# Four graph layers on one core: paired norm statistics, score dots from a PSUM copy, and new prices and offsets for the planner

## The chip, the core and the metric

The kernel runs on one core of a Trainium2 chip. The metric is the device time of one execution in microseconds; the time before is the median of three runs, 3304.65 us (3302.43 to 3311.59). A core has five instruction queues, which are named here as in the profile: PE (TensorE, matmuls; PEld are its weight loads), DVE (VectorE), ACT (ScalarE), POOL (GpSimd) and SP (SyncE, which issues the DMAs). SBUF is the working memory; PSUM is the memory that matmuls write, and DVE and ACT can read and write it too. The kernel uses PSUM as eight buffers of 128 x 512 float32.

## The reference, cut to what matters

`x` has the shape (128, 64, 512): 128 graphs of 64 nodes with 512 features. All numbers are float32. Each layer ends in a residual and a layer norm.

```python
def _layernorm(x, axis=-1, eps=1e-5):
    m = jnp.mean(x, axis=axis, keepdims=True)
    v = jnp.var(x, axis=axis, keepdims=True)
    return (x - m) / jnp.sqrt(v + eps)

# layer 0
out = deg[None, :, None] * (mi + b) + jnp.einsum('ij,bjo->bio', a, mj)
# layer 1: four attention heads, then one over the joined heads, then a feed-forward with its own norm
h = jax.nn.elu(_gat_heads(enc_inputs, adj, W_heads, a_heads))
...
out = jax.nn.elu(_gat_heads(h, adj, W_out[None], a_out[None])[:, 0])
ffn = jnp.maximum(out @ w1 + b1, 0.0) @ w2 + b2
y = ffn + out
...
return (y - mu) / jnp.sqrt(var + LN_EPS) * ln_gamma + ln_beta
# layers 2 and 3
Wh = jnp.einsum('bnd,de->bne', x, W)
e_src = jnp.einsum('bnd,d->bn', Wh, a_src)
e_dst = jnp.einsum('bnd,d->bn', Wh, a_dst)
logits = e_src[:, :, None] + e_dst[:, None, :]
logits = jnp.where(logits >= 0, logits, NEG_SLOPE * logits)
...
attn = jax.nn.softmax(logits, axis=-1)
attn = jnp.nan_to_num(attn, nan=0.0)
out = jnp.einsum('bnm,bmd->bnd', attn, Wh)
# the whole
x = _layernorm(x + layer(x, ...), axis=-1)      # for each of the four layers
```

## The kernel before, in words

The 128 graphs are 64 tiles of 128 rows (two graphs a tile). Two tiles make a *pair* (T = 2), so there are 32 pairs, p = 0 to 31, and 30 of them go in groups of two for the heads' matmuls. A pair's `x` stays in SBUF from the first layer to its output. Weights that are used again and again are streamed from DRAM (tiles named `ws_...`).

Matrix products are done by a seven-product scheme, `strassen` and `seven`: products gather in PSUM tiles `stx`, `sty` (and `stz` for the heads) and DVE adds them to the result in SBUF. Its operand sums (`s`, `s_o`, `s_y`, `t`) are POOL's. `seven` calls `whole(t)` when tile t of the result is whole: tile 0 after the fifth product, tile 1 after the seventh. There the norm of that tile begins.

A norm is `moments`, which is `bn_stats` and `bn_aggr` on DVE (tiles `st` and `mv`), then on POOL two operations on one column, the addition of epsilon and the power of -0.5 (tile `rs`). `normalize` adds DVE's shift `sh` = -mean x rs and one ACT instruction that scales and shifts the 128 x 512 tile. `norms` is the norm within layer 1 (its tiles end in `_1i`): moments, two DVE operations over 128 x 512 through a PSUM tile `ng`, then `normalize`.

Attention scores are dot products of a row of `x` with vectors that were multiplied through the weights beforehand, so no product Wh is needed for them. `dots` has DVE do them: for each of two vectors and two tiles one multiply-and-add over 128 x 512 (`tensor_tensor_reduce`, CUSTOM_DVE_ANT_0 in the profile, out to `j`) followed by the read of its accumulator into `f`. The vectors are broadcast to all partitions by DMA (`rows`). `stage_scores` does it for the four heads with four sets of rows, for pairs 2 to 31 (the first two pairs use matmuls); `stage_gat` for layers 2 and 3, for pairs 0 to 30; `stage_project` for `who`, the input of layer 1's second attention. `attention` then makes the softmax; in layers 2 and 3 the reciprocal `r` of the sum is multiplied by `has`, which is 0 for a node without neighbours.

The last pair runs by `stage_last` and `stage_tile`, a tile at a time with plain matmuls. The first six pairs (AHEAD) run layer 0 with plain matmuls too.

What sets the order is a planner. The stages are generators that note instructions (`Plan.note`) without issuing them; `yield 3.0` hands over to other stages for so much planned time. An instruction's rank is its place in the notes plus the offset of its kind from the table `LATER` (a kind is engine and tile, "te:stx"; "/S" is added for the first 11% of the notes, "/E" for the last 7%). `Plan.order` then simulates the five queues with a price for each instruction from `cost`: whenever an engine is free it takes the ready instruction of lowest rank. It also hands out tile buffers, the eight PSUM tiles (tag "b") among them, nearly in the order of the notes (NEAR). What comes out is the fixed order of each queue in the program; on the chip each engine goes through its queue in that order and waits where a result is not there. All instructions are issued by one line of `Plan.play`, L394, so the profile has one line for nearly everything and the tiles' names tell them apart.

Of the kernel before, what the change touches and what calls it, by code (L numbers as in the profile page):

```python
# [12 lines left out]
FP = mybir.dt.float32  # L13
BF = mybir.dt.bfloat16
I32 = mybir.dt.int32
AF = mybir.ActivationFunctionType
# [36 lines left out]
    "gp:aT": -137, "gp:aT/E": 66, "gp:aTg": 160, "gp:aTg/S": 321, "gp:ax": 238, "gp:ax/S": 124,  # L53
    "gp:bones": 54, "gp:bones/S": 51, "gp:fill": -170, "gp:fill/S": 66, "gp:gT": -160,
    "gp:gT/E": -163, "gp:gT/S": 4, "gp:hT": 400, "gp:hT/E": 72, "gp:hT/S": 5, "gp:hid": 64,
    "gp:hid/E": -203, "gp:hid/S": 44, "gp:ident": 138, "gp:ident/S": -93, "gp:mhalf": -400,
    "gp:mhalf/S": 96, "gp:never": 38, "gp:never/S": -5, "gp:o": 22, "gp:o/E": -95, "gp:o/S": 64,
    "gp:raw_W": -282, "gp:raw_W/S": 128, "gp:raw_w": -269, "gp:raw_w/S": -18, "gp:raw_wo": 15,
    "gp:raw_wo/S": 67, "gp:rs": 33, "gp:rs/S": 12, "gp:rs_i": 118, "gp:rs_i/E": -400,
    "gp:rs_i/S": 133, "gp:s": 32, "gp:s/E": -70, "gp:s/S": -46, "gp:s_o/E": -30, "gp:s_y": 75,  # L60
    "gp:s_y/E": -18, "gp:s_y/S": -25, "gp:t": -100, "gp:t/E": 179, "gp:t/S": -36, "gp:wh": -32,
    "gp:wh/S": 103, "gp:x": 43, "gp:x/E": -17, "gp:x/S": 27, "gp:ys": 11, "gp:ys/E": 148,
    "gp:ys/S": -271, "sc:a": -112, "sc:aT": 66, "sc:aT/E": 37, "sc:aT/S": -1, "sc:aT_o": 198,
    "sc:aT_o/E": 54, "sc:aTg": 38, "sc:aTg/E": 89, "sc:aTg/S": 62, "sc:a_h": -85,
    "sc:a_h/S": -114, "sc:ax": 275, "sc:ax/S": -233, "sc:bc": -55, "sc:elu": 278,
    "sc:elu/E": 69, "sc:elu/S": -88, "sc:f": -1, "sc:f/S": 15, "sc:gT": 70, "sc:gT/E": -33,
    "sc:hT": -218, "sc:hT/S": 107, "sc:hid": -42, "sc:hid/E": 137, "sc:o": 37, "sc:o/E": -40,
    "sc:o/S": -12, "sc:oT/E": -89, "sc:sm": -132, "sc:sm/E": -139, "sc:sm_o": -32,
    "sc:sm_o/E": 5, "sc:sm_o/S": 167, "sc:wat/S": 6, "sc:wat_h": 51, "sc:wat_h/S": -87,
    "sc:who": -33, "sc:who/E": 391, "sc:who/S": 29, "sc:x": -84, "sc:x/E": 51, "sc:xT": 14,  # L70
    "sc:xT/S": -265, "sc:ys": 30, "sc:ys/E": -17, "sc:ys/S": -86, "sy:W_last": -77,
    "sy:W_last/E": 157, "sy:adj_i": -224, "sy:adj_i/S": -45, "sy:b_sb": 129, "sy:b_sb/S": -118,
    "sy:beta": 215, "sy:beta/S": 13, "sy:d": 116, "sy:d/S": -6, "sy:d_W": -227, "sy:d_W/S": 130,
    "sy:d_W_T": -156, "sy:d_W_T/S": 60, "sy:d_f": 22, "sy:d_f/S": -11, "sy:d_h": 131,
    "sy:d_w": -353, "sy:d_w/S": -7, "sy:d_w_T": -12, "sy:d_w_T/S": 74, "sy:d_wh_S": -41,
    "sy:d_wh_S/S": 102, "sy:d_wo": -38, "sy:d_wo/S": -274, "sy:d_wo_T": -44, "sy:d_wo_T/S": 30,
    "sy:degb": -15, "sy:degb/S": 34, "sy:dram": -77, "sy:dram/E": -221, "sy:dram/S": -107,
    "sy:over": -119, "sy:over/S": 33, "sy:raw_W": -56, "sy:raw_W/S": 14, "sy:raw_w": -185,
    "sy:raw_w/S": 44, "sy:raw_wo/S": -31, "sy:rows": 93, "sy:rows/E": -108, "sy:rows/S": 25,
    "sy:rows_a": 215, "sy:rows_a/S": -76, "sy:rows_b": 103, "sy:rows_b/E": 40,  # L80
    "sy:rows_b/S": -25, "sy:rows_gamma": -33, "sy:rows_gamma/E": -72, "sy:rows_gamma/S": 16,
    "sy:rows_last": -88, "sy:rows_last/E": -8, "sy:rows_o": 20, "sy:rows_o/E": -138,
    "sy:rows_o/S": 155, "sy:w/S": -7, "sy:w_last": 79, "sy:w_last/E": -36, "sy:wh/S": 172,
    "sy:ws_W": 243, "sy:ws_W/E": -12, "sy:ws_W/S": 36, "sy:ws_W_T": -22, "sy:ws_W_T/E": 221,
    "sy:ws_W_T/S": 60, "sy:ws_w": 10, "sy:ws_w/E": 101, "sy:ws_w/S": 126, "sy:ws_w_T": 216,
    "sy:ws_w_T/E": -21, "sy:ws_w_T/S": -89, "sy:ws_wh/E": -21, "sy:ws_wh/S": -129,
    "sy:ws_wh_S": -11, "sy:ws_wh_S/E": 17, "sy:ws_wh_S/S": 55, "sy:ws_wo": 84, "sy:ws_wo/E": 82,
    "sy:ws_wo/S": 179, "sy:ws_wo_T": -360, "sy:ws_wo_T/E": -40, "sy:ws_wo_T/S": -18, "sy:x": 11,
    "sy:x/S": -43, "te:abd_ps": 3, "te:axp": 53, "te:axp/S": 27, "te:bc": -74, "te:bc/S": 33,
    "te:bc_o": -297, "te:bc_o/E": -9, "te:bc_o/S": -32, "te:fp": 6, "te:gp/E": 2, "te:gp/S": 93,  # L90
    "te:hidp": 76, "te:hidp/E": 16, "te:hidp/S": -39, "te:l": -109, "te:l/S": -1, "te:oTp": 40,
    "te:oTp/E": 137, "te:oTp/S": -205, "te:op": -253, "te:op/E": 178, "te:op/S": -50,
    "te:pt": -15, "te:pt/E": 54, "te:pt/S": -32, "te:pt_o": -73, "te:pt_o/E": -23,
    "te:pt_o/S": -97, "te:stx/E": 6, "te:stx/S": 21, "te:stx_h": -4, "te:stx_h/E": -109,
    "te:stx_o/E": 245, "te:stx_o/S": 10, "te:stx_y": 11, "te:stx_y/S": -26, "te:sty": 2,
    "te:sty/S": -20, "te:sty_h": -47, "te:sty_h/S": -27, "te:sty_o/E": -11, "te:sty_o/S": -29,
    "te:sty_y": -5, "te:sty_y/S": -4, "te:stz_h/E": 21, "te:wap": -29, "te:wap/S": 78,
    "te:wap_h": 279, "te:wap_h/S": -53, "te:xTp": 50, "te:xTp/S": 67, "te:yp/E": 1,
    "te:yp/S": -53, "te:z": -75, "te:z/E": 100, "ve:abd": -232, "ve:abd/S": 135, "ve:adj_f": 28,
    "ve:adj_f/S": 390, "ve:aggr": -6, "ve:aggr/S": 29, "ve:bc": -102, "ve:deg": 119,  # L100
    "ve:deg/S": -123, "ve:degb": 44, "ve:degb/S": 35, "ve:e/E": -129, "ve:e/S": -249,
    "ve:e_o": -169, "ve:e_o/E": 78, "ve:e_o/S": -70, "ve:f/E": 111, "ve:f/S": -25,
    "ve:f_o": -79, "ve:f_o/S": 51, "ve:gT/E": 18, "ve:gT/S": -17, "ve:hT": -8, "ve:hT/S": -210,
    "ve:has": -11, "ve:has/S": -98, "ve:ident": -122, "ve:ident/S": 48, "ve:mask": -266,
    "ve:mask/S": 177, "ve:mv": -35, "ve:mv/E": -83, "ve:mv/S": 86, "ve:mv_i": 209,
    "ve:mv_i/E": 80, "ve:mv_i/S": 142, "ve:mx": -67, "ve:mx/S": 22, "ve:ng": 35,
    "ve:ng/E": -118, "ve:ng/S": 67, "ve:nm/E": -141, "ve:nm/S": 33, "ve:nm_o": 133,
    "ve:nm_o/E": 277, "ve:nm_o/S": -302, "ve:o": 46, "ve:o/E": -35, "ve:o/S": 24,
    "ve:over": -105, "ve:over/S": -138, "ve:r": 91, "ve:r/E": -162, "ve:r/S": 83, "ve:r_o": -29,
    "ve:r_o/E": 45, "ve:r_o/S": 100, "ve:sh/S": 76, "ve:sm": 51, "ve:sm/S": -32, "ve:some": -51,  # L110
    "ve:some/S": -400, "ve:st": 14, "ve:st/E": -400, "ve:st/S": 39, "ve:st_i": -102,
    "ve:st_i/E": -38, "ve:wa": 4, "ve:wa_h": -52, "ve:wa_h/S": -53, "ve:who": 10, "ve:who/E": 4,
    "ve:who/S": -64, "ve:x": -230, "ve:x/E": -11, "ve:x/S": 47,
# [297 lines left out]
def cost(engine, name, args, kw, out):  # L411

    size = size_of(out)
    if engine == "tensor":
        if name == "transpose":
            return size * 0.00085, 0.0

        beside = P * P // math.prod(kw["lhsT"].shape)
        return (
            size * 0.00169 if beside == 1 else 0.208 / beside + 0.0003 * size  # L420
        ), 0.0
    if engine == "sync":
        return 0.06, 0.0015 * size
    if name == "tensor_tensor_reduce":
        return 0.7, 0.0
    if engine == "gpsimd":
        return 0.2 + 0.0021 * size, 0.0
    return 0.17 + (0.0011 if engine == "vector" else 0.00085) * size, 0.0
# [3 lines left out]
def gnn_stack_kernel(  # L432
# [92 lines left out]
    mhalf = cp.tile([P, 1], FP, tag="mhalf", name="mhalf")  # L525
# [268 lines left out]
    def moments(x, name):  # L794

        stats = small.tile([P, 6], FP, tag="stats", name=f"st_{name}")
        mv = small.tile([P, 2], FP, tag="mv", name=f"mv_{name}")
        nc.vector.bn_stats(stats, x)
        nc.vector.bn_aggr(mv, stats)
        rstd = small.tile([P, 1], FP, tag="rstd", name=f"rs_{name}")  # L800
        nc.gpsimd.tensor_scalar(rstd, mv[:, 1:2], EPS, None, ALU.add)
        nc.gpsimd.tensor_tensor(rstd, rstd, mhalf, ALU.pow)
        return mv[:, 0:1], rstd

    def normalize(x, name):

        mean, rstd = moments(x, name)
        shift = small.tile([P, 1], FP, tag="shift", name=f"sh_{name}")
        nc.vector.scalar_tensor_tensor(shift, mean, -1.0, rstd, ALU.mult, ALU.mult)
        nc.scalar.activation(x, x, AF.Identity, bias=shift, scale=rstd)  # L810

    def dots(f, x, rows, name):

        for s in range(2):
            for t in range(T):
                junk = unit.tile([P, D], BF, tag="junk", name=f"j_{name}_{s}_{t}")
                nc.vector.tensor_tensor_reduce(
                    junk, x[:, t, :], rows[:, s, :], 1.0, 0.0, ALU.mult, ALU.add,
                    accum_out=f(s, t),
                )  # L820

# [65 lines left out]
    def attention(f, alpha, mask, fill, has, name, T=T):  # L887
# [27 lines left out]
        if has is not None:  # L915
            nc.vector.tensor_scalar(r, r, has, None, ALU.mult)
# [569 lines left out]
```

## Time and profile before

| what | value |
|---|---|
| median of three runs | 3304.65 us |
| profiled execution, its span | 3308.7 us |
| instructions | 53,418 |
| mean granted clock of TensorE | 0.994 |
| POOL, the two rs operations, 256 each | 353 and 601 ns |
| the same in the inner norm, 64 each | 413 and 639 ns |
| DVE shift sh, 256 | 402 ns |
| ACT normalization of a tile, 256 | 812 ns |
| DVE alpha step of the attention, 128 x 128, layers 2 and 3, and in layer 1's second attention | 489 and 320 ns |
| DVE multiply of e by r, 128 x 128, layers 2 and 3 | 368 ns |
| DMA queue, share of 16 engines' span | 77.5% |

The profiled execution is one run of the program; times of groups are from it alone, and its span is 4 us above the median of the runs. In a line of a group, the two numbers after the bar are the busy time in us and the mean ns of one; then follow the idle time of the engine just before these instructions and what ended most of it. A matmul of float32 shows as two records, so the counts of PE are counts of records. A mean hides a spread: one line can be quick on a quiet stretch and slow on another.

### The profile page before, as it was taken

To read this page: it belongs to the slowest core of one execution; us is meant where nothing else is said; L and a number is where in the kernel's file an instruction comes from. 1 tells how busy PE (TensorE), PEld (TensorE's weight loads), DVE (VectorE), ACT (ScalarE), POOL (GpSimd) and SP (SyncE) were. 2 spreads that over 40 slices of the span, in tenths; PEclk is the share of its full clock that TensorE was granted. 3 is DMA by queue.
4 is the path that set the end of the run, shared out by engine and by line. 5 is a ranking of instruction groups with operands and counts; after the bars stand their busy time and mean duration, and the time that the engine had idled before them with its cause. 6 is when DMAs were issued, how large, how long until landed. Compare 5 with 4: busy or idle time off the path is not lost.

```text
span 3308.7 us, 53418 instructions
## 1 busy us (share of the span) xinstructions
PE 3234.1 (98%) x17860; PEld 2754.2 (83%) x17860; DVE 2313.0 (70%) x5480; ACT 1323.0 (40%) x2986; POOL 1652.5 (50%) x1794
## 2 busy tenths in 40 slices
PE   9999999999999999999999999999999999999997
PEld 5677888888888888888888888888888888878885
DVE  5876767767676776767767677676767767566666
ACT  3434334334433434334344443344344343433343
POOL 6754444455553544644455544555534454545433
PEclk9999999999999999999999999999999999999998
DMA  9896777878778787777878778787787877678772
GB/s 357 299 356 214 241 265 248 287 238 270 246 259 273 242 282 237 256 266 246 281 228 265 260 250 283 235 273 245 263 267 251 281 229 262 197 244 288 259 261 80
DMA packets 380702, 850.47 MB, mean 257 GB/s; under 512 B 42080, under 2 KB 58512, under 8 KB 380432
## 3 DMA queue, kind: packets, MB, share of 16 engines
q1 hardware_dynamic: 380432, 847.07, 77.5%
q8 instruction: 145, 2.38, 0.3%
q14 instruction: 125, 1.02, 0.1%
HBM read 806.13 MB, written 40.78 MB: 256 GB/s over the span
## 4 chain that ended last, share of the span: by engine, by line
PE 89%; DMA 6%; DVE 3%; issue 1%; POOL 1%; ACT 0%; SPq 0%; POOLq 0%; DVEq 0%
PE stx_h L394 13%; PE stx_o L394 12%; PE stx L394 11%; PE sty_o L394 9%; PE sty L394 8%; PE hidp L394 6%; PE stz_h L394 6%; PE sty_h L394 4%; PE yp L394 4%; PE gp L394 3%; DMA ws_wh<-d_wh 3%; PE stx_y L394 3%; PE l L394 3%; PE axp L394 2%; PE sty_y L394 2%; DVE j L394 1%
## 5 line engine op out<-in xcount | busy, mean ns | idle before, releaser
L394 DVE CUSTOM_DVE_ANT_0 j<-x,rows 128x512 bf16<-128x512 f32 x736 | 586.6, 797 | 64.1 <-DMA rows<-d 23.9
L394 POOL TENSOR_SCALAR rs<-mv 128x1 f32<-128x1 f32 x256 | 90.3, 353 | 549.8 <-DVE mv L394 538.0
L394 ACT COPY hT<-stx_h 128x512 f32<-128x512 f32 (+1 forms) x204 | 114.0, 559 | 548.1 <-PE stx_h L394 541.3
L394 ACT ACTIVATE x<-x,sh,rs 128x512 f32<-128x512 f32 x256 | 205.3, 812 | 249.8 <-DVE sh L394 249.3
L394 DVE TENSOR_TENSOR x<-stx,x 128x256 f32<-128x256 f32 x352 | 146.8, 419 | 176.4 <-PE stx L394 175.5
L394 PE MATMUL stx_h<-ys,ws_wh 128*128 128x256 f32 (+1 forms) x1088 | 247.0, 370 | 15.0 <-DMA ws_wh<-d_wh 14.6
L394 PE MATMUL sty_o<-ws_wo,hT 128*128 128x256 f32 x1024 | 246.3, 384 | 2.2 <-DMA ws_wo<-d_wo 2.2
L394 PE MATMUL stx_o<-ws_wo_T,s_o 128*128 128x256 f32 x1024 | 242.7, 380 | 2.3 <-DMA ws_wo_T<-d_wo_T 1.1
L394 PEld LDWEIGHTS stx_h<-ys,ws_wh 128*128 128x128 f32 x1088 | 195.6, 191 | 49.3 <-issue 16.8
L394 PE MATMUL hidp<-oT,w 128*128 128x256 f32 (+1 forms) x1056 | 233.8, 375 | 1.4 <-ACT oT L394 1.4
L394 ACT ACTIVATE elu<-hT 128x512 f32<-128x512 f32 x256 | 154.3, 603 | 187.8 <-DVE hT L394 184.7
L394 PEld LDWEIGHTS sty_o<-ws_wo,hT 128*128 128x128 f32 x1024 | 196.1, 193 | 29.7 <-issue 2.5
L394 PEld LDWEIGHTS hidp<-oT,w 128*128 128x128 f32 x1056 | 196.0, 192 | 28.2 <-ACT oT L394 2.0
L394 PEld LDWEIGHTS stx_o<-ws_wo_T,s_o 128*128 128x128 f32 x1024 | 190.1, 191 | 27.7 <-ACT e L394 1.5
L394 POOL TENSOR_TENSOR hid<-hid 128x256 f32<-128x256 f32 x31 | 22.7, 732 | 362.4 <-ACT hid L394 362.4
L394 DVE SCALAR_TENSOR_TENSOR hT<-elu,hT 128x512 f32<-128x512 f32 x256 | 174.6, 683 | 33.6 <-ACT elu L394 33.1
L394 DVE BATCH_NORM_STATS2 st<-x 128x6 f32<-128x512 f32 x256 | 176.3, 689 | 4.6
L394 POOL TENSOR_TENSOR rs<-rs,mhalf 128x1 f32<-128x1 f32 x256 | 153.9, 601 | 21.3
L394 ACT ACTIVATE elu<-elu 128x512 f32<-128x512 f32 x256 | 149.4, 583 | 6.8
L394 ACT COPY ys<-yp 128x512 f32<-128x512 f32 x256 | 134.3, 602 | 43.6 <-PE yp L394 42.9
L394 DVE SCALAR_TENSOR_TENSOR sh<-mv,rs 128x1 f32<-128x1 f32 x256 | 101.1, 402 | 71.6 <-POOL rs L394 70.8
L394 POOL TENSOR_TENSOR s<-gT 128x256 f32<-128x256 f32 x62 | 49.9, 804 | 200.6 <-DVE gT L394 197.2
(215 smaller groups left out, 7986.4 us busy)
## 6 DMA issues: line engine op xcount, KB each, us to landing
ws_wo_T<-d_wo_T SPq DMA_DIRECT2D x256, 512.0 KB, 4.8
ws_wo<-d_wo SPq DMA_DIRECT2D x192, 512.0 KB, 4.5
ws_wh_S<-d_wh_S SPq DMA_DIRECT2D x272, 256.0 KB, 4.1
ws_W_T<-d_W_T SPq DMA_DIRECT2D x248, 256.0 KB, 3.9
rows<-d_h SPq DMA_DIRECT2D x240, 256.0 KB, 4.2
ws_w_T<-d_w_T SPq DMA_DIRECT2D x104, 512.0 KB, 6.0
ws_wh<-d_wh SPq DMA_DIRECT2D x204, 256.0 KB, 4.8
ws_W<-d_W SPq DMA_DIRECT2D x186, 256.0 KB, 4.3
```

The lines of the kernel that those rows point to most:

```text
L394: getattr(getattr(self.tc.nc, s.engine), name)(*map(real, args), **{k: real(v) for k, v in kw.items()})
```

## The change

Six things are done.

1. `both`, `normalize_both` and `norms_both` are new. A pair's two tiles still get their own `bn_stats` and `bn_aggr` when each is whole, but into one tile `mv`; the epsilon, the power, and the shift are done once, over two columns, when the second tile is there. Then both tiles are normalized, one after the other. Layer 3's two output DMAs are issued after that. `moments` and `normalize` stay for the single tiles, with tiles of the new shape.
2. `seen` is new. It has ACT copy both tiles of `x` to PSUM, and the dots of `stage_scores` (pairs 2 to 31, one copy for all four sets of rows) and of `stage_gat` read `x` from there. `stage_project`'s dots go on reading `who` from SBUF, and `stage_tile`'s reading `x`.
3. `dots` goes over tiles in the outer loop and over the two vectors in the inner one, and its operands change places.
4. In `attention`, the multiplication of `r` by `has` and that of `e` by `r` become one instruction.
5. `cost` has new prices.
6. All of `LATER` is new, with "/M" for the notes between "/S" and "/E"; values lie between -500 and 500 (before: -400 to 400).

```diff
 LATER = {
-    "te:sty/S": -20, "te:sty_h": -47, "te:sty_h/S": -27, "te:sty_o/E": -11, "te:sty_o/S": -29,
...
+    "te:stx": -4, "te:stx/E": -71, "te:stx/M": 3, "te:stx/S": -372, "te:stx_h": -1,
+    "te:stx_h/E": 443, "te:stx_h/M": -18, "te:stx_h/S": -456, "te:stx_o": -34, "te:stx_o/E": -12,
+    "te:stx_o/M": 35, "te:stx_o/S": -25, "te:stx_y": -500, "te:stx_y/E": -367, "te:stx_y/M": 337,
...
 def cost(engine, name, args, kw, out):
 
     size = size_of(out)
+    views = [v for v in kw.values() if isinstance(v, View)]
+    ones = [v for v in [*args, *views] if isinstance(v, View) and math.prod(v.shape[1:]) == 1]
     if engine == "tensor":
...
         beside = P * P // math.prod(kw["lhsT"].shape)
-        return (
-            size * 0.00169 if beside == 1 else 0.208 / beside + 0.0003 * size
-        ), 0.0
+        if beside == 1:
+            return max(0.223, 0.0054 + size * 0.001667), 0.0
+        return (0.125 if beside == 2 else 0.27), 0.0
...
     if name == "tensor_tensor_reduce":
-        return 0.7, 0.0
+        held = any(isinstance(v, View) and v.tile.pool.space is PSUM for v in args)
+        return (0.77 if held else 0.86), 0.0
     if engine == "gpsimd":
-        return 0.2 + 0.0021 * size, 0.0
-    return 0.17 + (0.0011 if engine == "vector" else 0.00085) * size, 0.0
+        return 0.15 + 0.00235 * size + (0.25 if size == 1 else 0.0), 0.0
+    if engine == "scalar":
+        return 0.16 + 0.00085 * size + (0.1 * len(ones) if name == "activation" else 0.0), 0.0
+    return 0.15 + 0.00106 * size + (0.08 if ones else 0.0), 0.0
...
+    def both(x, name, then):
+
+        mv = small.tile([P, T, 2], FP, tag="mv", name=f"mv_{name}")
+
+        def whole(t):
+            stats = small.tile([P, 6], FP, tag="stats", name=f"st_{name}_{t}")
+            nc.vector.bn_stats(stats, x[:, t, :])
+            nc.vector.bn_aggr(mv[:, t, :], stats)
+            if t < T - 1:
+                return
+            rstd = small.tile([P, T], FP, tag="rstd", name=f"rs_{name}")
+            nc.gpsimd.tensor_scalar(rstd, mv[:, :, 1], EPS, None, ALU.add)
+            nc.gpsimd.tensor_tensor(rstd, rstd, mhalf, ALU.pow)
+            then(mv[:, :, 0], rstd)
+        return whole
+
+    def normalize_both(x, name, last=lambda t: None):
+
+        def then(mean, rstd):
+            shift = small.tile([P, T], FP, tag="shift", name=f"sh_{name}")
+            nc.vector.scalar_tensor_tensor(shift, mean, -1.0, rstd, ALU.mult, ALU.mult)
+            for t in range(T):
+                nc.scalar.activation(
+                    x[:, t, :], x[:, t, :], AF.Identity, bias=shift[:, t : t + 1],
+                    scale=rstd[:, t : t + 1],
+                )
+                last(t)
+        return both(x, name, then)
+
     def dots(f, x, rows, name):
 
-        for s in range(2):
-            for t in range(T):
+        for t in range(T):
+            for s in range(2):
                 junk = unit.tile([P, D], BF, tag="junk", name=f"j_{name}_{s}_{t}")
                 nc.vector.tensor_tensor_reduce(
-                    junk, x[:, t, :], rows[:, s, :], 1.0, 0.0, ALU.mult, ALU.add,
+                    junk, rows[:, s, :], x(t), 1.0, 0.0, ALU.mult, ALU.add,
                     accum_out=f(s, t),
                 )
 
+    def seen(x, name):
+
+        got = []
+        for t in range(T):
+            ps = psum.tile([P, D], FP, tag="b", name=f"seen_{name}_{t}")
+            nc.scalar.copy(ps, x[:, t, :])
+            got.append(ps)
+        return lambda t: got[t]
...
+        wide_r = r.unsqueeze(2).to_broadcast(bc3)
         if has is not None:
-            nc.vector.tensor_scalar(r, r, has, None, ALU.mult)
-        nc.vector.tensor_tensor(e, e, r.unsqueeze(2).to_broadcast(bc3), ALU.mult)
+            nc.vector.scalar_tensor_tensor(e, e, has, wide_r, ALU.mult, ALU.mult)
+        else:
+            nc.vector.tensor_tensor(e, e, wide_r, ALU.mult)
...
+    def norms_both(o, x, gamma_sb, name):
+
+        def then(mean, rstd):
+            whole = normalize_both(x, f"1_{name}")
+            for t in range(T):
+                ps = psum.tile([P, D], FP, tag="b", name=f"ng_{name}_{t}")
+                with nc.soon():
+                    nc.vector.scalar_tensor_tensor(
+                        ps, o[:, t, :], mean[:, t : t + 1], gamma_sb, ALU.subtract, ALU.mult
+                    )
+                    nc.vector.scalar_tensor_tensor(
+                        x[:, t, :], ps, rstd[:, t : t + 1], x[:, t, :], ALU.mult, ALU.add
+                    )
+                whole(t)
+        return both(o, f"1i_{name}", then)
...
+        if p >= 2:
+            held = seen(x, f"1_{p}")
...
                 dots(
                     lambda i, t: f[:, s, t * H + 2 * h2 + i : t * H + 2 * h2 + i + 1],
-                    x, r, f"1_{p}_{h2}_{s}",
+                    held, r, f"1_{p}_{h2}_{s}",
                 )
...
-            whole=lambda t: norms(o[:, t, :], x[:, t, :], gamma_sb, f"{p}_{t}"),
+            whole=norms_both(o, x, gamma_sb, f"{p}"),
...
-        dots(lambda s, t: f[:, s, t : t + 1], x, r, f"{name}_{p}")
+        dots(lambda s, t: f[:, s, t : t + 1], seen(x, f"{name}_{p}"), r, f"{name}_{p}")
...
-        def norm(t):
-            normalize(x[:, t, :], f"{name}_{p}_{t}")
+        def last(t):
             if name == "3":
                 nc.sync.dma_start(out=out[ts(p * T + t, P), :], in_=x[:, t, :])
...
-            f"{name}_{p}", 1.8, whole=norm,
+            f"{name}_{p}", 1.8, whole=normalize_both(x, f"{name}_{p}", last),
```

## The prediction

> **What bounds the kernel now.** I read the page's busy times first, then the price of an uninterrupted matmul in the chain of waits, then who TensorE waits for in the middle and at the end, then the groups that the change touches.
>
> ```profile
> span 3308.7 us, 53418 instructions
> PE 3234.1 (98%) x17860; PEld 2754.2 (83%) x17860; DVE 2313.0 (70%) x5480; ACT 1323.0 (40%) x2986; POOL 1652.5 (50%) x1794
> ```
>
> PE is busy for 98% of the span, and the next engine, DVE, for 70%. Busy is not the same as useful, since ends of matmuls are modelled, so I price the work. In the chain of waits these pieces run without a break:
>
> ```profile
> 2692.17 1.73 PE stz_h L394 x8
> 27.77 13.93 PE l L394 x32
> 2723.95 1.78 PE gp L394 x16
> 2677.57 1.99 PE yp L394 x32
> 2697.35 1.02 PE op L394 x8
> ```
>
> One record of 256 columns costs 1.73/8 = 0.216 us, one of 512 columns 13.93/32 = 0.435, a full one of 128 columns 1.78/16 = 0.111, a half-height one (yp, axp) 1.99/32 = 0.062, a quarter one (op) 0.128. The groups by shape count 11,996, 244, 2,223, 3,072 and 256 of them, and 69 small ones at about 0.11: 2594 + 106 + 247 + 191 + 33 + 8 = 3179 us. The span is 3308.7, so 130 us are lost in all. The same count by stage: 0 to 471 us loses 35; 471 to 2670 (eleven double turns of 199.9 us) loses 29; 2670 to 3190 loses 31; the last 119 us lose 34. Waits of TensorE in the middle have one cause, and it is small; the end is a set of short dependences:
>
> ```profile
> PE stx_h L394 <- DMA ws_wh<-d_wh: 11.3, 16, 2.2
> ```
>
> This is all that is listed between 470 and 2670 us (us in total, times, longest). After 3190 us the list is led by
>
> ```profile
> PE bc L394 <- DVE f L394: 4.9, 2, 4.1
> PE pt L394 <- DVE e L394: 1.8, 2, 1.3
> PE gp L394 <- ACT aTg L394: 1.8, 2, 1.1
> ```
>
> So TensorE sets the pace for two thirds of the time with 1.3% to spare (29/2199). Nothing that only relieves DVE, ACT or POOL can win there more than those 29 us. All work of TensorE stays as it is: its matmuls, tiles and weight streams are untouched.
>
> **The change part by part.** First the *score dots*.
>
> ```profile
> L394 DVE CUSTOM_DVE_ANT_0 j<-x,rows 128x512 bf16<-128x512 f32 x736 | 586.6, 797 | 64.1 <-DMA rows<-d 23.9 <-DMA rows<-d_h 21.1 <-ACT x L394 8.5
> L394 DVE CUSTOM_DVE_ANT_0 j_h<-wh,a_h 128x512 bf16<-128x512 f32 x32 | 21.8, 680 | 2.5 <-DMA wh<-in_W_heads_dram 1.3
> L394 ACT COPY a_h<-rows_a 128x512 f32<-128x512 f32 x8 | 4.7, 589 | 24.3 <-DMA rows_a<-in_a_heads_dram 12.8 <-DVE wa_h L394 11.5
> L394 DVE TENSOR_SCALAR r<-r,has 128x2 f32<-128x2 f32 x62 | 19.7, 318 | 2.1
> ```
>
> The columns are count, busy us, mean ns, idle before it. Of the 736 dots, 728 change (30 pairs x 16 for the heads, 31 x 8 for the two later layers; the last pair's 8 stay). The second row is the same operation with one operand in PSUM. 728 x (797 - 680) = 85 us of DVE are saved. Where DVE and POOL do not meet, the SBUF form is no slower: between 2000 and 2200 us its 48 instances run from 652 to 1635 ns with a median of 685. The saving is thus the long instances' own, and near the end, where POOL is 31% busy (37 of 119 us), I count none. Added are 30 x 2 + 31 x 2 x 2 = 184 copies on ACT, by the third row 0.59 us each: 108 us, taking ACT from 40% to 43%. On DVE 85 us are hidden behind TensorE, on ACT 108 also; without that cover, the copies would put 2 x 0.59 = 1.2 us ahead of each set of dots.
>
> [...]
>
> Second, *norm statistics*. 26 first-layer pairs, 31 norms of the feed-forward, 31 after it and 62 of the later layers go by pairs; 18 tiles (six early pairs, the last pair) and 2 inner norms stay single. POOL's two tiny operations cost 353 + 601 ns for a tile, 413 + 639 in the inner norm; 119 x 0.95 + 31 x 1.05 = 146 us fewer on POOL if a two-column operation costs what a one-column one does; no row shows one. Bounds: nothing more (tiny operations are mostly fixed cost), or twice the price, when POOL saves nothing. I take the first: 0.6 us is nearer to a fixed cost than to 128 x 512's 1.3 us divided by 512. DVE loses 119 shifts at 0.40: 48 us. The first tile's normalization now waits for the second's, two products (at least 1.7 us) later, on ACT and for layer 3 also its output DMA on SP's queue. Next stages read both tiles (gp's two tiles, the dots, the aggregation), so what ended last before still ends last: nothing on the path, up to 1.7 us once at the end if a tile's own output was last. Queued behind POOL's waiting operation are sums for strassen's operands (s, s_o, t), whose waiter is PE; POOL is 50% busy, so I take nothing in the middle.
>
> Third, the *has-multiply*. 62 instances of 0.318 us and 4 of 0.214 go, and the remaining multiply becomes a three-operand one: now 0.37 us, by the alpha step of the same shape 0.32 to 0.49. Net -0.2 to -0.3 us in a chain. About four such chains follow one another in the last 100 us: -1 us. There each set of dots for pair 30 also gets a copy ahead of it (+0.59 and a handover of some 0.2, less at most 4 x 0.12): +0.3 us twice. The three hand-made edits are worth -1 + 0.6, about nothing, on the path.
>
> Fourth, *prices and order*. The old prices had a dot at 0.70 us where the rows give 0.797 + 0.081 for its accumulator read; the new ones are 0.86, or 0.77 with PSUM. A POOL 128x512 add goes from 1.275 to 1.35 (rows: 1.28 to 1.46), half-height matmuls from 0.142 to 0.125 a pair of records (2 x 0.062). These are nearer to the trace; only POOL's two-column steps look underpriced (0.155 against 0.35 and 0.60). Then every kind of instruction on all five queues, weight loads on SP's too, gets a new offset. No row prices an order, so I bound it: at best it takes all the loss but the first 8 us and the 7 us from the last matmul (3301.8) to the end, -115 us; at worst TensorE waits as much again as now, by the page's list 62 us. Offsets of the frequent TensorE kinds stay small (stx -4+3, stx_h -1-18, stx_o -34+35), so the middle's pattern should survive; those of rare kinds sit at the limit of 500. I choose a quarter of the 130: 8 from the start, 7 from the middle (most of the ws_wh waits and what follows them), 15 from the last 640 us, where a shorter gap pays twice since the granted clock there is 0.91 against 1.00 in the middle. Sum: -30 us.
>
> Together 3308.7 - 30 = 3279 us on the profiled execution. That one lies 4 us over the median of 3304.65, so I forecast **3275**, with its own range of 3240 to 3294: from half the loss removed to just enough to be told.
>
> **The rivals.** *Hidden anyway*: the middle has no room, the ends are bound by dependences that every order has; 3304.65 - 2, between 3295 and 3315. For it speak the 98%; against it, 34 us lost in the last 119. *The order alone is worth much more*: half of all losses, 65 us and more, 3200 to 3240. For: the old planner underpriced 736 dots by 0.18 us and 128 by 0.11, some 146 us of DVE that it did not see. Against: DVE still was not what TensorE waited for in the middle. *Held banks*, on the slow side: all 8 PSUM banks share one ring, three strassen units take two or three each, and the heads' copy holds two of them through 16 dots, at least 16 x 0.77 = 12 us, longer when one of the four row loads (4.2 us to land) is late. If TensorE misses a bank for one batch of four dots, 3.1 us, in each of 30 pairs, that is +92 us, less the 30 of the order: 3367; for half a batch +46 - 30: 3321. It decides from 1.0 us per pair. For it: 12 us of two banks out of 8 in every 100. Against: no line of TensorE's waits in the middle is a release of a bank by DVE or ACT, so there is slack, and the planner counts banks. *Not what it says* (the dots as slow in PSUM) changes nothing in time, as they are hidden, and lies in the first rival.
>
> **How the numbers follow.** Forecast 0.55, much more 0.13, hidden 0.12, held banks 0.20. What a measurement here can tell from no change is 0.3%, 10 us: faster below 3294.7. Forecast and much more lie there, and hidden and held banks give a little to either side: faster 0.69, same 0.11, slower 0.20. The range starts at 3235, leaving out most of the third case, and runs to 3335, leaving out held banks of over 2 us a pair.
>
> **What would show it.** Right: dots near 0.69 us, 184 copies at 0.59, two-column rs operations below 0.7 us, a double turn still near 199 us, losses under 25 us before 471 and under 50 after 2670. Wrong: a double turn of over 201 us with TensorE waiting on DVE's j or on ACT's copies (held banks), or of 198 (much more), or POOL's two-column operations at twice the price. The prediction hangs on the order keeping the middle as tight as it is; a new wait of 1.5 us a pair there would undo it.

## The result, and the profile after

The changed kernel takes 3335.5 us (median of four runs, 3330.98 to 3346.53) against 3304.95 us before: a ratio of 1.0095, with an interval of 1.0076 to 1.0114. It is slower by 31 us; the forecast was 3275 us. The profiled execution after has a span of 3334.7 us, 26.0 more than before.

First the page's busy times and the chain of waits, after:

```profile
span 3334.7 us, 53080 instructions
PE 3252.0 (98%) x17860; PEld 2755.1 (83%) x17860; DVE 2176.1 (65%) x5295; ACT 1412.4 (42%) x3170; POOL 1460.5 (44%) x1494
PE 83%; DVE 8%; DMA 7%; issue 1%; POOL 1%; ACT 0%; SPq 0%; POOLq 0%; ACTq 0%; DVEq 0%
```

TensorE has the same 17,860 records. DVE lost 137 us of work, POOL 192, ACT gained 89, and none of it came back: relief for engines that were already hidden. What grew is TensorE's own loss. With the prediction's prices its work is 3179 us in both, and what is left over was counted in three windows:

| window of the span, us | lost before | lost after |
|---|---|---|
| 0 to 470 | 35.6 | 31.2 |
| 470 to 2670 | 29.6 | 53.6 |
| 2670 to the end | 65.0 | 71.4 |

The start gained 4, the end lost 6, and the middle lost 24: there a double turn went from 199.9 to 202.2 us. The groups that were edited did mostly what the prediction said (by shape; busy us, mean ns, idle before):

```profile
L422 DVE CUSTOM_DVE_ANT_0 j<-rows,seen 128x512 bf16<-128x512 f32 x728 | 495.6, 681 | 66.9 <-DMA rows<-d_h 43.9 <-ACT seen L422 9.5 <-DMA ws_wh_S<-d_wh_S 3.3
L422 ACT COPY seen<-x 128x512 f32<-128x512 f32 x184 | 104.8, 586 | 0.5
L422 POOL TENSOR_SCALAR rs<-mv 128x2 f32<-128x2 f32 x119 | 30.4, 256 | 426.6 <-DVE mv L422 425.0 <-DVE sh L422 1.0 <-DVE mv_1i L422 0.6
L422 POOL TENSOR_TENSOR rs<-rs,mhalf 128x2 f32<-128x2 f32 x119 | 90.2, 758 | 9.9
L422 DVE SCALAR_TENSOR_TENSOR e<-e,has,r 128x128 f32<-128x128 f32 x62 | 38.1, 615 | 2.1
```

Dots at 0.681 us and 184 copies at 0.586 are as worked out. A pair's two rs operations cost 256 + 758 = 1014 ns, near the 954 of one tile, so pairing nearly halves them; in the inner norm a pair costs 477 + 830 = 1307 ns, where one tile cost 1052. The joined multiply costs 0.615 us here, more than the 0.49 that I had set as its upper price.

The waits of TensorE between 470 and 2670 us (in total, times, longest) are more kinds than the single one before:

```profile
PE sty_h L422 <- DMA ws_wh<-d_wh: 11.0, 9, 1.7
PE pt L422 <- DVE e L422: 2.7, 10, 0.3
PE stx_y L422 <- DMA ws_w_T<-d_w_T: 2.5, 4, 1.4
PE sty_y L422 <- DVE f L422: 0.8, 1, 0.8
PE sty_y L422 <- DMA ws_w_T<-d_w_T: 0.7, 1, 0.7
PE sty_o L422 <- POOL x L422: 0.5, 1, 0.5
PE sty_y L422 <- DMA ws_w<-d_w: 0.3, 1, 0.3
```

They add 7 us (18.5 against 11.3), and 24 have to be found. The rest sits in pieces that no wait names. TensorE's queue before (start, length, what) has its matmuls on 64 rows (axp and yp) in long groups:

```profile
960.63 1.16 PE L394 MATMUL axp<-aggr,x 64*128 64x128 f32 x16
961.63 1.95 PE L394 MATMUL yp<-aT,x 64*128 64x128 f32 x32
963.51 1.99 PE L394 MATMUL stx_o<-ws_wo_T,hT 128*128 128x256 f32 x8
```

This is a stretch of the chain of waits after (start, length, what), where they stand in shorter groups:

```profile
973.15 1.73 PE stx L422 x8
974.88 0.86 PE sty L422 x4
975.74 1.09 PE yp L422 x16
976.83 1.06 PE stx L422 x4
977.89 0.86 PE sty L422 x4
978.76 1.09 PE yp L422 x16
```

Four records of stx or sty take 0.86 us, and 1.06 just after a yp group. Sixteen of yp take 1.09, where the prediction's half-height price makes 16 x 0.062 = 1.0. yp, axp and op are matmuls on 64 of the 128 rows; the others are full-height. So I took the start of each group of records, less the start of the group before it and less that group's records at their price, over the middle of both kernels. The prices are the prediction's, but 0.0605 us for a half-height record, which makes two such groups that follow one another come out at nothing. What is over the price is lost time:

```
from -> to, 470 to 2670 us     before: count, us over      after: count, us over
full -> full, no wait            1434    8.1                1363    9.9
full -> full, behind a wait        16   13.9                  26   22.2
full -> half, no wait              77    8.1                 117   13.0
half -> full, no wait              77    2.8                 116   10.8
half -> full, behind a wait         0                          1    0.7
half -> half, no wait              50   -0.1                  11    0.3
```

Waits cost 9 us more, changes of height, 233 and not 154, 12.9 us more (0.16 us for each further one), and the other groups 2 us more: 24 in all, the middle's loss. A new group of the same height costs next to nothing without a wait (6 to 7 ns each), so it is the height and not the change of group. In the whole program TensorE's queue has 248 changes before and 338 after: the new order scatters the half-height groups.

### The profile page after: what moved, and what is told of

Its sections match the earlier page's. It is cut to its first block, busy times and chain, and to the rows that moved or that the text cites. A ratio compares the mean times of both kernels' runs of the same rounds, so it can differ in the third digit from the quotient of the medians.

```text
span 3334.7 us, 53080 instructions
## 1 busy us (share of the span) xinstructions
PE 3252.0 (98%) x17860; PEld 2755.1 (83%) x17860; DVE 2176.1 (65%) x5295; ACT 1412.4 (42%) x3170; POOL 1460.5 (44%) x1494
## 4 chain that ended last, share of the span: by engine, by line
PE 83%; DVE 8%; DMA 7%; issue 1%; POOL 1%; ACT 0%; SPq 0%; POOLq 0%; ACTq 0%; DVEq 0%
PE stx_h L422 11%; PE stx L422 11%; PE stx_o L422 11%; PE sty L422 8%; PE sty_o L422 7%; PE hidp L422 6%; PE stz_h L422 5%; PE sty_h L422 4%; PE yp L422 4%; PE gp L422 3%; PE stx_y L422 3%; PE l L422 2%; PE sty_y L422 2%; DMA ws_wh<-d_wh 2%; DVE bc L422 2%; PE axp L422 1%
## 5 line engine op out<-in xcount | busy, mean ns | idle before, releaser
L422 DVE CUSTOM_DVE_ANT_0 j<-rows,seen 128x512 bf16<-128x512 f32 x728 | 495.6, 681 | 66.9 <-DMA rows<-d_h 43.9
L422 POOL TENSOR_SCALAR rs<-mv 128x2 f32<-128x2 f32 (+1 forms) x137 | 34.7, 253 | 481.8 <-DVE mv L422 480.1
L422 DVE TENSOR_TENSOR x<-sty,x 128x256 f32<-128x256 f32 (+1 forms) x176 | 97.1, 555 | 149.9 <-PE sty L422 133.5
L422 POOL TENSOR_TENSOR hT<-hT,s_o 128x512 f32<-128x512 f32 x64 | 86.6, 1353 | 231.6 <-PE sty_o L422 231.5
L422 POOL TENSOR_TENSOR ys<-ys,t 128x512 f32<-128x512 f32 (+1 forms) x68 | 82.5, 1213 | 183.5 <-PE sty_h L422 183.4
```

What stands on the lines that cost most here:

```text
L422: getattr(getattr(self.tc.nc, s.engine), name)(*map(real, args), **{k: real(v) for k, v in kw.items()})
```

## The experiments

**Program and order, crossed.** The first question was whether the edits or the new order lose the time. The theories were *order* (prices and offsets), *held banks* (the prediction's slow rival) and *fragile fit* (offsets fit one program only).

```diff
 # edits_old_order: the changed kernel
-LATER, cost: as changed
+LATER, cost: as before
 # new_order_alone: the kernel before
-LATER, cost: as before
+LATER, cost: as changed
```

> The changed kernel with the prices and the table of offsets of before: the three hand-made edits alone. Theory 'order' (the new prices and offsets lose the time in the middle, the edits are hidden): 3295 to 3312 us, a double turn of about 199.5 us. Theory 'held banks' (the PSUM copies hold two of eight banks, and TensorE runs closer to its evacuations): 3330 us or more, a double turn of about 202 us. Theory 'fragile fit' (offsets fit one program only; whatever shifts the notes loses the fit): 3315 to 3340 us.

> The kernel before with the new prices and offsets alone, dots from SBUF, norms single. Theory 'order': 3330 to 3345 us, the middle losing 4 to 5 us in a double turn. Theory 'held banks': 3295 to 3310 us, since no bank is held. Theory 'fragile fit': 3330 us or more, since the new offsets were not made for this program.

Measured: 3411.99 us (ratio 1.0334, 1.0318 to 1.0349) and 3501.34 us (1.0604, 1.0587 to 1.0621). Each half alone is far worse than both together:

| | prices and offsets of before | new prices and offsets |
|---|---|---|
| program before | 3302 to 3305 | 3501 |
| edited program | 3412 | 3336 |

Against the 3302.2 of the runs beside them they cost 110 and 199 us. If the two added, both together would take 3611; measured is 275 less. So a program and its table of offsets are one thing, and neither theory of a single guilty half holds. Of the losses of the two unfitted kernels in the middle (101 and 151 us), 62 and 96 us stand behind waits of TensorE.

```diff
 # after_dots_sbuf: the changed kernel, planned anew
-            held = seen(x, f"1_{p}")
+            held = lambda t: x[:, t, :]
...
-        dots(lambda s, t: f[:, s, t : t + 1], seen(x, f"{name}_{p}"), r, f"{name}_{p}")
+        dots(lambda s, t: f[:, s, t : t + 1], lambda t: x[:, t, :], r, f"{name}_{p}")
 # before_nudged: the kernel before
-    "te:bc": -74,
+    "te:bc": -60,
```

> The changed kernel without the PSUM copies: dots read x from SBUF, all else as changed. Theory 'order': 3330 to 3345 us. Theory 'held banks': back to 3310 us or less, a double turn under 200 us. Theory 'fragile fit': 3335 us or more.

> The kernel before with one of its offsets moved from -74 to -60 (te:bc, a transpose of two columns in the attentions). Theories 'order' and 'held banks': 3302 to 3310 us, as nothing of weight changes. Theory 'fragile fit': 3315 us or more, since one moved instruction shifts all that is planned after it.

Measured: 3477.44 us (1.0536, 1.0516 to 1.0556) without the copies, 3303.49 us (1.0005, 0.9995 to 1.0014) with the nudge. Leaving instructions out of the notes breaks the fit; this one small move of one offset, which changed places in every compute queue, does not. So *fragile fit* as I wrote it is too strong; how large a move of offsets it takes was not tried.

**One edit, planned anew and in place.** To see an edit's own price, the order must be held. The joined has-multiply was put in twice: into the notes, and at the time of issue, when all queues stand.

```diff
 # before_has: in attention(), as in the change
-            nc.vector.tensor_scalar(r, r, has, None, ALU.mult)
-        nc.vector.tensor_tensor(e, e, r.unsqueeze(2).to_broadcast(bc3), ALU.mult)
+            nc.vector.scalar_tensor_tensor(e, e, has, wide_r, ALU.mult, ALU.mult)
 # before_has_fixed: in play(), after the planning
                 for name, args, kw in s.calls:
+                    if name == "tensor_scalar" and s.kind == "ve:r":
+                        self.has[id(args[0].tile)] = args[2]
+                        continue
+                    if name == "tensor_tensor" and id(getattr(args[2], "tile", 0)) in self.has:
+                        has = self.has[id(args[2].tile)]
+                        name, args = "scalar_tensor_tensor", (args[0], args[1], has, args[2], ALU.mult, ALU.mult)
```

> The kernel before with one hand-made edit, the joined has-multiply, planned anew with the prices and offsets of before. Its 66 small DVE operations fewer are hidden or gain 1 us at the end. Theory 'fragile fit' (whatever shifts the notes loses the fit of the offsets): 3330 to 3360 us. Theory 'only large edits break the fit': 3300 to 3310 us.

> The same edit, but put in when the instructions are issued, after the planning, so that all five queues keep the order of before and only lose the 66 operations. Both theories: 3298 to 3306 us, the edit itself costs nothing. If it is over 3310, the three-operand multiply or its wait costs time by itself and the fit is not to blame.

Measured: 3346.82 us (1.0135, 1.0110 to 1.0159) and 3297.13 us (0.9990, 0.9975 to 1.0004). The edit costs nothing; taking 66 tiny operations out of the notes cost 45 to 47 us, by the order alone. The joined multiply itself, in the order of before:

```profile
L401 DVE SCALAR_TENSOR_TENSOR e<-e,has,r 128x128 f32<-128x128 f32 x62 | 26.9, 433 | 2.1
```

It takes 433 ns here, 615 in the changed kernel and 544 in `after_fixed_sbuf` below, with the changed kernel's order: one price does not hold in all three, and with the order of before it lies in the range that the prediction gave.

**The PSUM copies, with the order held.** The same method on the changed kernel: the dots read what the copy copied, so the values are the same.

```diff
 # after_fixed_sbuf, in play(); after_fixed_nocopy also has the marked line
                 for name, args, kw in s.calls:
+                    if name == "copy" and s.kind == "sc:seen":
+                        self.source[id(args[0].tile)] = args[1]
+                        continue                     # after_fixed_nocopy only
+                    if name == "tensor_tensor_reduce" and id(getattr(args[2], "tile", 0)) in self.source:
+                        args = (*args[:2], self.source[id(args[2].tile)], *args[3:])
```

> The changed kernel with its order kept as it is; only the dots read x in SBUF where the copy took it from, so that a copy's PSUM bank is free as soon as it is written, and the dots go back to the slower form. Theory 'held banks' (30 us of the changed kernel are TensorE's want of banks): 3315 us or less, a double turn near 200 us. Theory 'order' (the new order itself runs TensorE closer to what feeds it): 3328 to 3345 us. If the PSUM reading of the dots was a gain that matters: over 3345.

> As the run with the dots in SBUF and the order kept, with the 184 copies on ACT left out as well: ACT loses 108 us of work and no bank is taken. Theory 'held banks': 3315 us or less, as there. Theory 'copies' (ACT's copies delay its evacuations, and TensorE through them): 3315 or less here alone, and 3330 or more with the copies. Theory 'order': 3325 to 3345 in both.

Measured: 3352.25 us (1.0150, 1.0129 to 1.0171) and 3352.68 us (1.0153, 1.0132 to 1.0175). The dots' line of the first, by shape:

```profile
L427 DVE CUSTOM_DVE_ANT_0 j<-rows,x 128x512 bf16<-128x512 f32 x728 | 587.7, 807 | 52.9 <-DMA rows<-d_h 41.5 <-ACT x L427 2.6
```

The dots go back from 681 to 807 ns and the kernel loses 17 us. All of the longer mean lies in 145 instances of over 720 ns, each of which overlaps with a POOL instruction; the medians are 685 and 679 ns, and no dot from PSUM takes over 691. *Held banks* falls: a bank freed at once brings nothing. The slower dots alone could hide a small gain from it, but TensorE's waits of the changed kernel name no copy and no `j`; the nearest, on DVE's `f`, is 0.8 us. *Copies* falls too, since 105 us less on ACT change nothing. The PSUM dots are a gain in this order, about 0.5%.

**Changes of height.** With banks and copies out, the excess table above was the lead. For its price, the kernel before got 198 more changes with no work added.

```diff
 # before_more_switches, in play(): s and t are neighbours in TensorE's queue, one half-height, one full
+    calls += [(s, c) for c in s.calls[:-n]] + [(t, c) for c in t.calls[:k]]
+    calls += [(s, c) for c in s.calls[-n:]]
+    t.calls = t.calls[k:]
```

> The kernel before, same work and same order of all queues, but at 99 places where TensorE goes from a full-height group of matmuls to a half-height one or back, the last matmul of the first group and the first of the second change places: 198 more changes between the two heights. Theory 'switches' (a change of height costs TensorE 0.07 to 0.11 us, by the excess time at such places, and the new order has 338 of them against 248): 3314 to 3324 us. If a change costs nothing of its own: 3298 to 3306 us.

Measured: 3345.1 us (1.0122, 1.0107 to 1.0137), that is 40 us for 198 changes, 0.20 us each, twice what I expected. Its queue of TensorE (start, length, what) shows the pieces:

```profile
1064.80 1.46 PE L430 MATMUL stx_h<-ys,ws_wh 128*128 128x256 f32 x6
1066.18 0.49 PE L430 MATMUL axp<-aggr,x 64*128 64x128 f32 x4
1066.61 0.70 PE L430 MATMUL stx_h<-ys,ws_wh 128*128 128x256 f32 x2
1067.23 0.94 PE L430 MATMUL axp<-aggr,x 64*128 64x128 f32 x12
...
1078.18 0.49 PE L430 MATMUL pt<-ident,e 128*128 128x128 f32 x3
1078.60 0.49 PE L430 MATMUL yp<-aT,x 64*128 64x128 f32 x4
1079.03 0.33 PE L430 MATMUL pt<-ident,e 128*128 128x128 f32 x1
```

From 1066.18 to 1066.61 four half-height records take 0.43 us, 0.25 by their price; from 1066.61 to 1067.23 two full ones take 0.62, 0.43 by theirs. Each change costs 0.18 to 0.19 at this place, and no line has an idle time. By the count of the table above, the middle of this run has 280 changes that cost 33.3 us, against 154 and 10.9 before: 0.18 us for each further one. TensorE's waits in the middle stay what they were:

```profile
PE stx_h L430 <- DMA ws_wh<-d_wh: 12.9, 17, 2.2
PE sty_h L430 <- DMA ws_wh<-d_wh: 0.3, 1, 0.3
```

The counter-test is the changed kernel with fewer of them. I moved its offsets on until its own planner's end stayed equal (3309 us planned, 3310 as changed) at 282 changes.

```diff
 # after_fewer_switches: 535 offsets moved, among them
-    "sc:ys/M": -162, "te:yp": -15, "te:yp/M": 44, "te:axp/M": 500
+    "sc:ys/M": -548, "te:yp": 1, "te:yp/M": 34, "te:axp/M": 463
```

> The changed kernel with some of its offsets moved further, chosen so that the planner's own end stays where it was (3309 planned, 3310 as changed) while TensorE's queue changes 282 times between half-height and full-height groups and not 338 times. Theory 'switches' (0.2 us for a change, by the run with 198 more of them): 56 x 0.2 = 11 us less, 3320 to 3328 us. Theory 'order, but not by its switches': 3331 to 3340 us.

Measured: 3322.64 us (1.0064, 1.0050 to 1.0077). Each of its runs is below each of the changed kernel's, though the two intervals just touch; by the ratios it is 10 us less. That this fits 56 x 0.2 is in part luck: its profiled execution is 14 us shorter, 7 us in the middle, where 53 of the 56 changes went, and 7 us after 2670 us, where three did. By the same count as above, changes of height in the middle fell from 23.8 us (and 0.7 at one with a wait) to 14.8 (and 3.0 at three), while full-height groups behind a wait stayed at 22.2. So the middle gained 0.13 us a change in all. The gain at the end is that of another part of the order, since 535 offsets moved.

One pair of numbers fits all four kernels. Take whole stretches of half-height records (yp and axp) without a wait, from the record before a stretch to the record after it, 4 to 64 records long: with 0.0556 us a record, the way in and out costs 0.29 to 0.35 us together, whatever the length, so some 0.15 us a change. The 0.0605 of the table hides part of this where stretches are long, as before. A change of height then costs 0.15 us by the stretches and 0.20 by the time of the run with 198 more of them.

**Two runs on the rest.** Pairing in place: every two-column operation issued as two.

```diff
 # after_fixed_unpaired, in play()
+                    if s.kind in ("gp:rs", "gp:rs_i", "ve:sh") and args[0].shape[1] == T:
+                        for t in range(T):
+                            getattr(getattr(self.tc.nc, s.engine), name)(*[
+                                real(a[:, t : t + 1] if isinstance(a, View) else a) for a in args
+                            ])
+                        continue
 # before_refit: 530 offsets moved, among them
-    "sc:ys": 30, "te:sty_y": -5
+    "sc:ys": 338, "te:sty_y": -67, "te:sty_y/M": -120
```

> The changed kernel with its order kept; each two-column operation of the norms (epsilon, power, shift) is issued as two one-column ones in its place. POOL gets the 300 tiny operations back, DVE 150 shifts. If pairing is worth something in this order: 3340 to 3360 us. If it is hidden: 3330 to 3340 us. It cannot tell what the later start of the first tile costs, since the place stays.

> The kernel before, none of the edits and its own prices, with offsets moved further until the planner's own end fell from 3337 to 3317, at 246 changes of height (248 before). If the planner's clock ranks two orders of one program rightly when the changes of height are equal: 3278 to 3292 us, which beats both kernels. If it does not rank orders this close: 3296 to 3312 us.

The unpaired one took 3344.91 us (1.0123, 1.0101 to 1.0145): some 9 us over the changed kernel, but the intervals touch, so pairing's gain in this order stays likely and not shown. With the order kept, the one-column operations take 234 and 568 ns, so that a pair saves 0.59 us of POOL. The refitted kernel of before took 3302.13 us (1.0004, 0.9995 to 1.0012): the planner saw 20 us less, the chip none. No version here beats the kernel before beyond its interval. Large losses the planner does see. Its own ends, each by its own prices, are 3337 us for the kernel before and 3310 for the changed one. For the four kernels that lost most when planned anew they are:

| kernel | planned, us | measured, us |
|---|---|---|
| before_has | 3380 | 3347 |
| edits_old_order | 3434 | 3412 |
| after_dots_sbuf | 3496 | 3477 |
| new_order_alone | 3499 | 3501 |

## Why the prediction was wrong

- **What bounds it** was right: TensorE sets the pace, the middle can win little, and relief of DVE and POOL is mostly hidden. The warning that a new wait of 1.5 us a pair in the middle would undo it was near in size: the middle lost 24 us over 22 pairs, 1.1 each. Only 9 of the 24 stand behind waits.
- **Score dots**: the price and the sign were right (681 ns against 680 expected). So was the reading that the saving is that of the long instances alone. That the 85 us would be wholly hidden was not: with the order held they are worth 17 us.
- **Norm statistics**: the price was right within 60 ns a pair, and 255 ns too low in the 31 inner norms; the power alone, 758 ns, is above the 0.7 us that was named as the sign of being right. **Has-multiply**: the price was right in the order of before (433 ns, in 320 to 490) and too low in the new one (615), without effect on the time in place. The handover of some 0.2 us ahead of the dots, in the sum of the edits, no run shows: in the changed kernel the 16 dots whose wait ends with a copy start 32 to 33 ns after its end.
- **Prices and order** is the step that failed. I wrote "I choose a quarter of the 130" and made it -30 us on the path. Its sign was wrong. With the queues kept, taking the PSUM dots, the copies or the pairing back out of the changed kernel makes it slower or changes nothing, so the 31 us lie with its order. For the last 640 us I had let a shorter gap pay twice, by a granted clock of 0.91: that is the clock before of the last 119 us alone, the 640 have 0.97, and that a gap pays twice no run shows; after the one wait of 7.6 us below, sixteen records take 2.7 us more than is usual. By stage, the start gave 4 of its 8 us; the middle was to gain 7, mostly from the waits for `ws_wh`, but these stayed (11.3 and 11.0 us) and it lost 24; the end was to gain 15 and lost 6. I had priced the order by the waits that it could remove, and held the new prices to be a gain because they were "nearer to the trace". But 0.125 us for a pair of half-height records is one price for every place; what it costs to go from one height to the other, 0.15 to 0.20 us, no price in the planner, old or new, knows. 90 more changes come to 14 to 18 of the 31 us.
- **The sum**: I added the edits and the order as independent terms. The crossed runs show that they are not: alone they cost 110 and 199 us, together 31.
- **Held banks**, the slow rival that I gave 0.20, fell; the slow side came by a mechanism that was in none of the rivals. A double turn of over 201 us, its sign, did come, but without a wait on `j` or on the copies. That the time lies at the slow end of the range, which stood for this rival, is chance. "The middle's pattern should survive" because the frequent offsets are small was an argument from the table, not from the queue's order.

For the rest, 13 to 17 us, the trace has two candidates, neither tried alone: the 9 us more behind waits in the middle, and one long wait at the end. In TensorE's queue after:

```profile
2999.44 2.06 PE L422 MATMUL axp<-aggr,x 64*128 64x128 f32 x32
3009.05 3.78 PE L422 MATMUL stx_o<-ws_wo_T,s_o 128*128 128x256 f32 x8 [7.56 <-DVE who L422]
3012.62 2.76 PE L422 MATMUL sty_o<-ws_wo,hT 128*128 128x256 f32 x8
```

Before, TensorE's longest wait for `who` was 1.1 us. Here it is 7.6, and the eight records after it take 3.6 us to the next start, where 1.73 is usual, and the next eight 2.6: from 3004 to 3014 us the granted clock is 0.51. The start's gain of 4 us stands against it. In the run with fewer changes of height the longest wait for `who` is 2.7 us, and its loss after 2670 us is 64.4, as before (65.0). Which part of the new order makes DVE late there stays open.

## What to carry to other kernels

Where a hand-written or searched order keeps the bounding engine at 98%, an edit's price and the price of planning it anew are two measurements: hold the queues and put the edit in at issue for the first. A planner's own end warns of a loss of 45 us and more, but is no forecast between orders this close: 27 us less planned were 31 more on the chip, and 20 less planned were none. And look at what the bounding engine loses between instructions without a wait: here half of it was in the starts of groups, not in its busy time or its list of waits.

## What the runs showed of the hardware

- A change between matmuls on 64 rows and on 128 rows costs TensorE 0.15 to 0.20 us in float32 (40 us for 198 changes; 0.15 by the stretches in four traces), without any idle time in the profile. The runs show a cost at such changes and its size; what causes it, none shows.
- DVE's dots read a PSUM operand in 681 ns and two SBUF operands in 807 ns on the mean with the same order of queues. The medians are 679 and 685 ns; the difference is that of the 145 instances that overlap with a POOL instruction and take over 720 ns. In the kernel before it is 151 of 736, each beside a POOL instruction too, and the other 585 have a mean of 682 ns. Of these 585, 177 overlap with POOL too, so overlap alone does not make a dot long; what does, no run shows.
- A two-column power on POOL takes 758 ns (changed kernel) against 568 for one column (`after_fixed_unpaired`, same order of queues). The multiply by `has` and the broadcast `r` in one DVE operation takes 433 ns for 128 x 128 in the order of before, against 368 for the multiply by `r` alone, and 615 in the changed kernel.
